# Gate and up units of a feed-forward stage: two of seven products replaced by seven half-size ones, computed one unit ahead

## The chip, the cores and the metric

The kernel runs on one NeuronCore of one Trainium2 chip. The metric is the device time of one execution in microseconds (us). Engines are named as in the profile: PE is the matrix engine, PEld its weight loads, DVE the vector engine, ACT the scalar engine, POOL and SP the two engines that issue most of the transfers here.

## The reference, cut to what matters

The input is 2048 tokens of 512 features, all in f32. One RWKV-like block (time mix, then channel mix) is followed by a gated feed-forward part, and the change lies in the latter:

```python
def _L0_ffn_ref(h_shard, w_gate_up, w_down):
    gate_up = jnp.einsum('bsh,oh->bso', h_shard, w_gate_up)
    gate, up = jnp.split(gate_up, 2, axis=-1)
    h = jax.nn.silu(gate) * up
    out = jnp.einsum('bsi,hi->bsh', h, w_down)
    return out
...
x = x + _L0_attn_ref(_layernorm(x, axis=-1), ...)
x = x + _L0_ffn_ref(_layernorm(x, axis=-1), w_gate_up, w_down)
```

Gate and up have 2048 columns each, so each is four 512 x 512 matrices; down goes from 2048 back to 512.

## The kernel before

Tokens are handled in four blocks of 512. A *unit* is one 512 x 512 weight matrix times one block. It is made with a Strassen-Winograd scheme: weights and activations are cut into 2 x 2 quarters of 256 x 256, sums of quarters are formed (S1 to S4 of the weights, T1 to T4 of the activations), and seven products of quarters replace eight. The seven are, as weight and activation: A11 B11, A12 B21, S2 T2, S1 T1, S3 T3, S4 B22, A22 T4. Each product is four PE matmuls with a 128 x 128 weight and 256 moving columns, and takes one weight tile of 256 KB, which SP loads into `wring`, a ring of 12 tiles, ahead of its use.

`unit` (matmul at L602) runs the products on PSUM banks: `z`, taken from the pool `ps` of six banks, is accumulated over A11 B11, S2 T2, S1 T1, S3 T3 and A22 T4, and read in between; `accv` and `accx` are two banks of their own. ACT copies partial results out (L622 into `accv`, L633 into `u2`, L637 into `accx`), DVE adds them, and `sink` takes each finished quarter: for a gate unit ACT's Silu into a tile `s` (L1169), for an up unit DVE's product with `s` into `hid`. The last three products are not run at once: they go into the list `held`, and the next unit or stage places them between its own products.

The order of all instructions on PE, DVE and ACT is the order in which the Python code issues them. `tick` is called after each product: it counts what DVE has been given, and while there is slack it issues steps of background work: the next block's normalization and transposes (`ffn_in`), sums of hidden quarters (`hidden_done`, `quarter_sums`), and the weight sums (`prepare`). A weight matrix's four sums are prepared once: POOL loads four raw quarters from DRAM, DVE forms S1 to S4, POOL stores them (`prepare`, `prep_one`, `credit`, `pause`); the list `late` gives the order. DVE works in order, so a sum whose raw quarter has not landed holds up what is behind it.

The feed-forward part runs block by block, with gate and up units in turn (`ffn_gate`, `ffn_up`, g = 0 to 3), the next block's first gate unit, and then `ffn_down`. Down uses the scheme twice, one inside the other (`down_product`): 49 products, each of four matmuls with 128 moving columns (L1342). The feed-forward part covers about the span from 655 us to its end.

Of the kernel before, what the change touches and what calls it, by code (L numbers as in the profile page):

```python
# [15 lines left out]
P = 128  # L16
# [4 lines left out]
HB = TB // 2  # L21
# [42 lines left out]
def rwkv_ffn_kernel(  # L64
# [20 lines left out]
    up = ctx.enter_context(tc.tile_pool(name="up", bufs=10))  # L85
    prep = ctx.enter_context(tc.tile_pool(name="prep", bufs=6))
    small = ctx.enter_context(tc.tile_pool(name="small", bufs=3))
    ps = ctx.enter_context(tc.tile_pool(name="ps", bufs=6, space=bass.MemoryType.PSUM))
    pv = ctx.enter_context(tc.tile_pool(name="pv", bufs=1, space=bass.MemoryType.PSUM))
    px = ctx.enter_context(tc.tile_pool(name="px", bufs=1, space=bass.MemoryType.PSUM))  # L90
    dram = ctx.enter_context(tc.tile_pool(name="dram", bufs=1, space=bass.MemoryType.DRAM))


# [16 lines left out]
        return tokp.tile([P, NT, H], F32, tag="tok", name=name)  # L110

    def bank():
        return ps.tile([P, 2, HB], F32, tag="ps", name="ps")

# [29 lines left out]
    def value_part(q, k):  # L146

        if q < 4:
            return wv[q, k].rearrange("p (g c) -> p g c", c=P)
        m, kk = divmod((0, 1, 3, 2)[k], 2)  # L150
        return vsum[q - 4][:, :, kk, m * P : (m + 1) * P]

    for q in (A11, A12, A22, S1, S2, S3, S4):
        sources["vv", q] = [value_part(q, k) for k in range(4)]
# [63 lines left out]
    def value_weight(q, k):  # L218
# [9 lines left out]
        nc.sync.dma_start(t, value_part(q, k))  # L228
        return t

    def load_x(b, queues=None):
        t = tok_tile("x")
        for k in range(NT):
            eng = queues[k] if queues else nc.sync
            paced(eng.dma_start(t[:, k, :], x_t[b][:, k, :]))
        return t
# [54 lines left out]
    preps = deque()  # L291
    credit = [0.0, 0.0]
    pause = [WAIT]

    def prep_one():
        item = preps[0]
        if item[1] > 0:
            return False
        try:
            if next(item[2]) is not None:  # L300
                item[1] = pause[0]
        except StopIteration:
            preps.popleft()
            finished.add(("sums", item[0]))
            if len(preps) > 1 and item[3] > 1:
                begin(preps[1])
            elif preps:
                begin(preps[0])
        return True
# [7 lines left out]
    def prepare_all(ns, own, depth):  # L317
        empty = not preps
        for n in ns:
            preps.append([n, 0, prepare(n, own), depth, False])  # L320
        if empty:
            for item in list(preps)[:depth]:
                begin(item)
# [106 lines left out]
    def tt(out, a, b, op):  # L430
        nc.vector.tensor_tensor(out, a, b, op)  # L431
        cost(size(out))
# [150 lines left out]
    def unit(weights, Bs, sink, by_token, done=None, free=None):  # L583
# [86 lines left out]
        for s in order:  # L670
            if s is None:
                pop_held()
            else:
                s()
                tick()
        held.extend(((STEP, step7), (STEP, step3), (STEP, step4)))

    def plain_unit(n, B, sink, by_token, done=None, free=None, halfway=None, hold=False):

# [451 lines left out]
    def ffn_in(b):  # L1131
# [24 lines left out]
        finished.add((b, "z"))  # L1156
        yield 1
        yield from sums_of(B)

    gated = {}  # L1160

    def ffn_gate(b, g):
        s = gated[b, g] = {}

        tile_of = q_tile if g % 2 else u_tile

        def sink(i, j, c):
            t = tile_of("s")
            nc.scalar.activation(t, c, AF.Silu)  # L1169
            s[i, j] = t  # L1170

        unit([WG + g], [Lazy((b, "z"))], sink, False)

    def ffn_up(b, g):
        s = gated.pop((b, g))
        hid = hidden.setdefault(b, {})

        def sink(i, j, c):
            q = (B11, B12, B21, B22)[2 * i + j]
            if q not in hid:  # L1180
                hid[q] = hidden_tile()
            tt(hid[q][:, g], c, s[i, j], ALU.mult)
            if g == 3:
                made.add((b, q))
                if q in (B11, B22):
                    quarter_sums(b, 0 if q == B11 else 1)

        unit(
            [WU + g],
            [Lazy((b, "z"))],  # L1190
            sink,
            False,
            lambda: hidden_done(b, g),
            op_done if g == 3 else None,
        )
# [38 lines left out]

    def last_room():
        middle.close()
        pools["q"] = ctx.enter_context(
            tc.tile_pool(name="fq", bufs=4, reuse_waits="tile")
        )

    def quarters(t):
        return {2 * k + m: t[:, :, k, m * P : (m + 1) * P] for k in range(2) for m in range(2)}
# [212 lines left out]

    early = [WV, WCR, WO] + [WKEY + g for g in range(4)] + [WVAL, WVAL + 1]
    late = [("vv", q) for q in (A11, S4, S2, A12, S1, S3, A22)]
    late += [n + g for g in range(4) for n in (WG, WU)] + [("dd", A11)]
    late += [("d", k) for k in range(4)] + [("dd", q) for q in (S4, S2, A12, S1, S3, A22)]

    ctx.enter_context(
        tc.manual_schedule(
# [25 lines left out]
    for b in range(NB):  # L1488
# [3 lines left out]
        if b == NB - 1:  # L1492
            load_resid(0)
        if b >= DEEP:
            credit[1], pause[0] = 1.0, LONG
        gate_unit(b)
        if b + 1 < NB:
            out_unit(b + 1)
# [32 lines left out]
                u(b + 2)  # L1531
    credit[1] = 0.75
    need((0, "z"))
    ffn_gate(0, 0)
    last_room()
    for b in range(NB):
        for g in range(4):
            if g > 0:
                need((b, "z"))
                ffn_gate(b, g)  # L1540
            if g == 0 and b + 1 < NB:
                load_resid(b + 1)
            ffn_up(b, g)
            if g == 1 and b + 1 < NB:
                push((b + 1, "z", "t"), ffn_in(b + 1), op_free)
        if b + 1 < NB:
            need((b + 1, "z"))
            ffn_gate(b + 1, 0)
        ffn_down(b)
# [80 lines left out]
```

## Time and profile before

| | |
|---|---|
| median of three runs | 1232.89 us (1231.09 to 1233.88) |
| profiled execution, its own time | 1231.09 us |
| its span, first to last instruction | 1229.0 us |
| PE busy | 1219.5 us, 99% of the span |
| DVE busy | 780.3 us, 63% |
| ACT busy | 368.4 us, 30% |
| moved by DMA | 319.03 MB, mean 260 GB/s |
| granted PE clock | 1.000 |

The page of a profile gives busy time by engine, the span in 40 slices, the chain of work that ended last, and the costliest groups of instructions; a group is a line of the kernel, an engine, an operation and its tiles. A helper that issues all additions (`tt`, L431) gives its line to all of them, so DVE is read by tiles.

### The profile page before, as it was taken

What the parts mean: (1) busy time and instruction counts of PE and PEld (TensorE: products, weight loads), DVE (VectorE), ACT (ScalarE), POOL (GpSimd) and SP (SyncE); (2) the same over time, 40 slices, a digit from 0 to 9 for tenths busy, and PEclk for the clock granted to TensorE, in tenths of its full rate; (3) what the DMA queues carried; (4) which work ended last, traced back from release to release, by engine and by line L of the source; (5) the groups of instructions that cost most, each with busy time, mean ns of one, the idle gap of its engine ahead of it and who ended that gap; (6) DMA issues with size and microseconds to landing.
All of it is one profiled execution on the core that took longest, in us unless ns stands there. A gap on an engine that the chain in (4) does not pass through costs nothing.

```text
span 1229.0 us, 19201 instructions
## 1 busy us (share of the span) xinstructions
PE 1219.5 (99%) x6860; PEld 1106.3 (90%) x6860; DVE 780.3 (63%) x1451; ACT 368.4 (30%) x713; POOL 186.6 (15%) x334
## 2 busy tenths in 40 slices
PE   9999999999999999999999999999999999999998
PEld 8888888888888888998899888998899888998898
DVE  5877686577685666886775577646546364553466
ACT  5534252242532333323412222112221232112211
POOL 2232221223212222002201222200000000000000
PEclk9999999999999999999999999999999999999999
DMA  5768985899888988899889978995469745785576
GB/s 196 250 221 282 319 299 206 302 320 302 277 262 270 312 288 263 261 297 381 280 281 329 335 232 279 362 343 154 146 194 309 258 143 153 250 290 154 153 225 204
DMA packets 159620, 319.03 MB, mean 260 GB/s; under 512 B 19096, under 2 KB 32552, under 8 KB 158248
## 3 DMA queue, kind: packets, MB, share of 16 engines
q1 hardware_dynamic: 132000, 230.22, 58.4%
q0 software_dynamic: 25920, 84.96, 19.0%
q10 hardware_dynamic: 1608, 2.65, 0.7%
q8 instruction: 55, 0.90, 0.3%
q14 instruction: 37, 0.30, 0.1%
HBM read 268.46 MB, written 49.29 MB: 259 GB/s over the span
## 4 chain that ended last, share of the span: by engine, by line
PE 90%; DVE 4%; DMA 3%; ACT 2%; issue 1%; POOL 1%; ACTq 0%; DVEq 0%; POOLq 0%
PE ps L602 45%; PE ps L1342 21%; PE accx L602 9%; PE accv L602 9%; PE ps L704 5%; DMA raw<-in_w 2%; PE ps L487 1%; DMA vsum<-raw 1%; DMA row<-stats 1%; ACT mix L540 1%; DVE raw L431 0%; DVE e L439 0%; DVE h L435 0%; DVE st L445 0%; POOL raw L181 0%
## 5 line engine op out<-in xcount | busy, mean ns | idle before, releaser
L602 PE MATMUL ps<-zT,w 128*128 128x256 f32 x1280 | 289.3, 380 | 0.0
L602 PEld LDWEIGHTS ps<-zT,w 128*128 128x128 f32 x1280 | 242.4, 191 | 31.5
L602 PE MATMUL ps<-mix,w 128*128 128x256 f32 x920 | 211.1, 380 | 1.3 <-ACT u L633 1.3
L602 PEld LDWEIGHTS ps<-mix,w 128*128 128x128 f32 x920 | 174.3, 190 | 24.5 <-ACT u L633 1.7
L1342 PE MATMUL ps<-w,hid 128*128 128x128 f32 x1248 | 156.8, 275 | 0.0
L1342 PEld LDWEIGHTS ps<-w,hid 128*128 128x128 f32 x1248 | 149.7, 192 | 1.2
L1342 PE MATMUL ps<-w,quads 128*128 128x128 f32 x1056 | 133.5, 276 | 0.4 <-ACT r L1354 0.4
L1342 PEld LDWEIGHTS ps<-w,quads 128*128 128x128 f32 x1056 | 126.4, 192 | 1.1 <-ACT r L1354 0.5
L1354 ACT COPY r<-ps 128x128 f32<-128x128 f32 x168 | 44.5, 265 | 204.5 <-PE ps L1342 201.9
L431 DVE TENSOR_TENSOR raw<-raw 128x512 f32<-128x512 f32 x120 | 82.5, 688 | 30.9 <-issue 11.1
L431 DVE TENSOR_TENSOR u<-u,accx 128x512 f32<-128x512 f32 x64 | 43.8, 685 | 85.7 <-ACT accx L637 85.7
L431 DVE TENSOR_TENSOR hid<-hid 128x512 f32<-128x512 f32 x126 | 84.9, 687 | 2.0 <-ACT hid L1068 0.3
L622 ACT COPY accv<-ps 128x512 f32<-128x512 f32 x64 | 36.5, 571 | 158.0 <-PE ps L602 155.2
L637 ACT COPY accx<-ps 128x512 f32<-128x512 f32 x64 | 36.5, 570 | 132.7 <-PE ps L602 126.2
L431 DVE TENSOR_TENSOR u<-ps,u 128x512 f32<-128x512 f32 x64 | 44.2, 690 | 44.5 <-PE ps L602 40.6
L704 PE MATMUL ps<-mix,w 128*128 128x256 f32 x320 | 70.8, 380 | 1.1 <-DVE mix L439 1.1
L633 ACT COPY u<-ps 128x512 f32<-128x512 f32 x64 | 37.4, 584 | 109.5 <-PE ps L602 109.5
L704 PEld LDWEIGHTS ps<-mix,w 128*128 128x128 f32 x320 | 60.4, 191 | 9.5 <-DVE mix L439 1.8
L431 DVE TENSOR_TENSOR r<-ps,r 128x256 f32<-128x256 f32 x83 | 29.8, 359 | 51.5 <-PE ps L1342 47.1
L602 PE MATMUL accv<-zT,w 128*128 128x256 f32 x256 | 60.6, 380 | 0.0
L602 PE MATMUL accx<-zT,w 128*128 128x256 f32 x256 | 60.5, 380 | 0.0
L602 PE MATMUL ps<-w,t 128*128 128x256 f32 x264 | 59.4, 379 | 0.0
(179 smaller groups left out, 1593.7 us busy)
## 6 DMA issues: line engine op xcount, KB each, us to landing
w<-sum SPq DMA_DIRECT2D x248, 256.0 KB, 4.2
w<-in_w SPq DMA_DIRECT2D x230, 256.0 KB, 4.2
w<-dd SPq DMA_DIRECT2D x112, 256.0 KB, 3.8
w<-vsum SPq DMA_DIRECT2D x56, 256.0 KB, 4.4
w<-vv SPq DMA_DIRECT2D x56, 256.0 KB, 4.0
raw<-in_w POOLq DMA_DIRECT2D x48, 256.0 KB, 6.7
w<-d SPq DMA_DIRECT2D x48, 256.0 KB, 3.5
sum<-raw POOLq DMA_DIRECT2D x40, 256.0 KB, 4.1
```

Of the source, the lines that this page charges most:

```text
L431: nc.vector.tensor_tensor(out, a, b, op)
L487: nc.tensor.transpose(flat[:, t * P : (t + 1) * P], h[:, t, c * P : (c + 1) * P], ident)
L540: nc.scalar.activation(dst(c), hT[:, c, 0:TB].rearrange("p (j t) -> p j t", j=2), AF.Copy, scale=onem[:, row - MK, c : c + 1],)
L602: mm = nc.tensor.matmul(pz[:, m, :], lhsT=lhsT, rhs=rhs, start=first and g == 0 and m == 0 and k == 0, stop=g == last and k == 1, skip_gro ...
L622: "z", A11, B11, True, pop_held, read=lambda: nc.scalar.copy(accv, acc["z"])
L633: nc.scalar.copy(tmp["u2"], acc["z"])
L637: nc.scalar.copy(accx, acc["z"])
L704: mm = nc.tensor.matmul(acc[i, j][:, m, :], lhsT=act[:, k, lo] if by_token else wg[:, k, lo], rhs=wg[:, k, :] if by_token else act[:, k, : ...
L1342: mm = nc.tensor.matmul(dst, lhsT=x[k][:, g, :], rhs=wt[:, g, :], start=first and g == 0, stop=g == 3, skip_group_check=True,)
L1354: nc.scalar.copy(st["r"][:, m, n * P : (n + 1) * P], st["z"])
```

## The change

Of the gate and up units, all but the first gate and the first up of block 0 get their A11 B11 and S3 T3 from a new function, `inner`. Instead of two products of four matmuls with 256 moving columns it makes seven of the same scheme one level down, each with half the size: two matmuls with 128 moving columns, one for A11 B11 and one for S3 T3, which lie side by side in a bank. The seven go into two banks of `ps` (`z`: A11, S2, S1, S3, A22; `y`: A12, S4), are read into a tile `pair` by ACT (`keep`) and joined by DVE (`joined`, and an addition in `five`). They are cut into five steps (`one` to `five`), and `paired_unit` places one (a call of `small`) in front of each of its own products, one unit ahead: while unit u runs its five remaining products, it makes the two results that unit u+1 needs. At its end ACT writes the finished A11 B11 of the next unit from `pair` into the banks `z` and `accv`, where the next unit's products add to it; S3 T3 (`plus`) is added by DVE when a quarter is taken. Only one product (`last`: S4 B22) is held over.

Around it: `z` and a new bank `w` become fixed banks (`acc2`), for which `ps` is left with four banks in the feed-forward part; inner sums of the activations are formed by DVE (`inner_sums`), inner sums of the weights by four more `prepare` items (`("in", ...)`); each inner step needs four weight tiles in place of two; a prepare item's loads may begin while the one before it is at work (`AHEAD`); `ffn_in` of the next block is pushed one pair of units earlier; the order `late`, and some credits, change.

The core of the diff:

```diff
-    ps = ctx.enter_context(tc.tile_pool(name="ps", bufs=6, space=bass.MemoryType.PSUM))
     pv = ctx.enter_context(tc.tile_pool(name="pv", bufs=1, space=bass.MemoryType.PSUM))
     px = ctx.enter_context(tc.tile_pool(name="px", bufs=1, space=bass.MemoryType.PSUM))
+    ps = ctx.enter_context(tc.tile_pool(name="ps", bufs=4, space=bass.MemoryType.PSUM))
+    extra = ctx.enter_context(ExitStack())
+    banks = [
+        ps,
+        ps,
+        extra.enter_context(tc.tile_pool(name="ps2", bufs=2, space=bass.MemoryType.PSUM)),
+    ]
...
+        banks.append(banks.pop(0))
+        return banks[-1].tile([P, 2, HB], F32, tag="ps", name="ps")
...
+    def inner_weight(n, q):
+        t = WG if n < WU else WU
+        need_sums(("in", t, q))
+        r = wring.tile([P, 2, HB], F32, tag="w", name="w").rearrange("p a (h c) -> p (a h) c", c=P)
+        nc.sync.dma_start(r, insums[t, q][:, :, n - t, :])
+        return r
...
+            item[5] += 1
+            if item[5] == AHEAD[0] and item[3] == 1 and len(preps) > 1:
+                begin(preps[1])
...
+        def act(i, k):
+            wanted = ("in", tcol[k]) if k in tcol else T3
+            while wanted not in B["sums"]:
+                run_one(True)
+            if k in tcol:
+                return B["in"][:, i, tcol[k], :]
+            k, j = divmod(k, 2)
+            return B[(B11, T3)[i]][:, k, j * P : (j + 1) * P]
...
+        def mm(dst, q, k, start):
+            for i in range(2):
+                m = nc.tensor.matmul(
+                    dst[:, i, :],
+                    lhsT=wt(i, q),
+                    rhs=act(i, k),
+                    start=start and i == 0,
+                    stop=True,
+                    skip_group_check=True,
+                )
+            latest[:] = [m.ins.name]
+        def keep(m, j):
+            nc.scalar.copy(st["r"][:, :, m, j * P : (j + 1) * P], st["z"])
+        def one():
+            st["r"] = pair_tile()
+            st["w"] = [weight(n, A11), weight(n, S3)]
+            st["s"] = [inner_weight(n, A11), inner_weight(n, S3)]
+            st["z"] = flat(bank())[:, :HB].rearrange("p (i c) -> p i c", i=2)
+            st["y"] = bank().rearrange("p i (j c) -> p i j c", j=2)
+            mm(st["z"], A11, B11, True)
+            keep(0, 0)
+            mm(st["y"][:, :, 0, :], A12, B21, True)
+            tick(2 * HALF)
+        def two():
+            mm(st["z"], S2, T2, False)
+            keep(1, 0)
+            tick(HALF)
+        def three():
+            mm(st["z"], S1, T1, False)
+            keep(0, 1)
+            mm(st["y"][:, :, 1, :], S4, B22, False)
+            later(joined, 1)
+            tick(2 * HALF)
+        def joined():
+            r = st["r"]
+            tt(r[:, :, 1, :P], r[:, :, 1, :P], r[:, :, 0, P:], ALU.subtract)
+            tt(
+                r[:, :, 0, :],
+                st["y"].rearrange("p i j c -> p i (j c)"),
+                r[:, :, 0, :],
+                ALU.add,
+            )
+        def four():
+            mm(st["z"], S3, "T3", False)
+            keep(1, 1)
+            tick(HALF)
+        def five():
+            mm(st["z"], A22, T4, False)
+            r = st["r"]
+            tt(r[:, :, 1, :P], st["z"], r[:, :, 1, :P], ALU.add)
+            tick(HALF)
...
+        z, aw = acc2["z"], acc2["w"]
+        plus = None if st is None else st["r"][:, 1]
+        u2 = None
+        small()
+        pop_held()
+        if st is None:
+            product(z, A11, B11, True)
+            nc.scalar.copy(accv, z)
+            tick()
+            pop_held()
+        small()
+        product(z, S2, T2)
+        if st is None:
+            u2 = u_tile("u2")
+            nc.scalar.copy(u2, z)
+        else:
+            nc.scalar.copy(aw, z)
+        tick()
+        pop_held()
+        small()
+        product(accv, A12, B21)
+        sink(0, 0, accv)
+        tick()
+        if st is None:
+            plus = bank()
+            product(plus, S3, T3, True)
+            tt(u2, plus, u2, ALU.add)
+            plus7 = u_tile("p7")
+            nc.scalar.copy(plus7, plus)
+            plus = plus7
+            tick()
+        small()
+        product(z, S1, T1)
+        nc.scalar.copy(accx, z)
+        sink(1, 1, z, plus)
+        tick()
+        small()
+        product(aw, A22, T4, st is None)
+        sink(1, 0, aw, plus if u2 is None else u2)
+        if after is not None:
+            r = ahead[after[0]][0]["r"][:, 0]
+            nc.scalar.copy(z, r)
+            nc.scalar.copy(accv, r)
+        tick()
+        def last():
+            product(accx, S4, B22)
+            sink(0, 1, accx)
+            if free is not None:
+                free()
+            if done is not None:
+                later(done, 1)
+        held.append((STEP, last))
...
+        sums = (
+            (x(0, 1), x(0, 0)),
+            (x(1, 1), new[:, :, 0, :]),
+            (x(1, 0), new[:, :, 1, :]),
+            (x(1, 1), x(0, 1)),
+        )
+        for k, (i0, i1) in enumerate(sums):
+            tt(new[:, :, k, :], i0, i1, ALU.subtract)
+            B["sums"].add(("in", k))
+            yield
...
+        def sink(i, j, c, plus=None):
+            t = u_tile("s")
+            if plus is not None:
+                tt(t, c, plus, ALU.add)
+                c = t
             nc.scalar.activation(t, c, AF.Silu)
             s[i, j] = t
-        unit([WG + g], [Lazy((b, "z"))], sink, False)
+        if (b, g) == (0, 0):
+            unit([WG + g], [Lazy((b, "z"))], sink, False)
+            return
+        paired_unit((b, g, 0), b, WG + g, following(b, g, 0), sink)
...
+            h = hid[q][:, g]
+            if plus is not None:
+                tt(h, c, plus, ALU.add)
+                c = h
+            tt(h, c, s[i, j], ALU.mult)
...
-    late += [n + g for g in range(4) for n in (WG, WU)] + [("dd", A11)]
-    late += [("d", k) for k in range(4)] + [("dd", q) for q in (S4, S2, A12, S1, S3, A22)]
+    late += [n + g for n in (WG, WU) for g in range(4)]
+    late += [("in", n, q) for q in (A11, S3) for n in (WU, WG)] + [("dd", A11)]
+    late += [("d", k) for k in range(4)] + [("dd", q) for q in (A12, S4, S2, S1, S3, A22)]
...
-            credit[1], pause[0] = 1.0, LONG
+            credit[1], pause[0], AHEAD[0] = 0.75, LONG, 2
...
+    banks[:] = [ps]
...
-            if g == 1 and b + 1 < NB:
+            if g == 0 and b + 1 < NB:
                 push((b + 1, "z", "t"), ffn_in(b + 1), op_free)
+            credit[1] = 0.45 if g in (0, 1) else 0.75
```

In `joined` the sums of the scheme's second level are formed; `following` names the next gate or up unit, `None` after the last one, and gates alternate with ups except where a down stage lies between.

## Prediction

> **What bounds the kernel now.** I read the page's head and its chain first, to see which engine sets the end.
>
> ```profile
> PE 1219.5 (99%) x6860; PEld 1106.3 (90%) x6860; DVE 780.3 (63%) x1451; ACT 368.4 (30%) x713; POOL 186.6 (15%) x334
> PE 90%; DVE 4%; DMA 3%; ACT 2%; issue 1%; POOL 1%; ACTq 0%; DVEq 0%; POOLq 0%
> ```
>
> PE is busy 99% of the span and makes 90% of the chain. A microsecond less of PE work is a microsecond of the end, as long as PE does not begin to wait. The chain in order of time, at the end of block 2's units, shows what each product costs (start, length, line, records; a product is 8 records).
>
> ```profile
> 1026.24 1.73 PE accv L602 x8
> 1027.97 1.73 PE ps L602 x8
> 1043.51 3.45 PE ps L602 x16
> 1046.97 0.89 PE ps L1342 x8
> 1047.86 1.73 PE ps L602 x8
> ```
>
> A product with 256 moving columns takes 1.727 us (accv to ps: 1027.97 - 1026.24), one with 128 takes 0.893 us (39.30 us for the 352 records from 1054.83). A unit is seven of the former, 12.09 us, with no gap. Then the timeline (start, length), for how soon a reader starts, and for PE after a wait:
>
> ```profile
> 963.90 1.89 PE L602 MATMUL accv<-zT,w 128*128 128x256 f32 x8
> 964.10 0.69 DVE L431 TENSOR_TENSOR hid<-ps,s 128x512 f32<-128x512 f32 x1 [2.17 <-PE ps L602]
> 965.63 1.89 PE L602 MATMUL ps<-zT,w 128*128 128x256 f32 x8
> 965.89 0.60 ACT L1169 ACTIVATE s<-accv 128x512 f32<-128x512 f32 x1 [2.94 <-PE accv L602]
> ```
>
> Counted from the start of PE's next product, DVE reads the last one's result after 0.20 us, ACT after 0.26. Where PE waited for ACT (423.95 us, 1.29 us of waiting) it restarted 0.05 us after ACT's copy ended. Groups by form give the other durations, and the windows the DMA (20 us each; the last two numbers are the busy share and GB/s).
>
> ```profile
> L622 ACT COPY accv<-ps 128x512 f32<-128x512 f32 x64 | 36.5, 571 | 158.0 <-PE ps L602 155.2
> L1169 ACT ACTIVATE s<-u 128x512 f32<-128x512 f32 x16 | 10.1, 632 | 8.6 <-DVE u L431 8.6
> L836 ACT COPY row<-ps 4x256 f32<-4x256 f32 x2 | 0.7, 358 | 0.0
> L431 DVE TENSOR_TENSOR u<-ps,u 128x512 f32<-128x512 f32 x64 | 44.2, 690 | 44.5 <-PE ps L602 40.6
> L431 DVE TENSOR_TENSOR r<-ps,r 128x256 f32<-128x256 f32 x42 | 17.9, 425 | 4.4
> ```
>
> ```profile
> 560.00:580.00 20.00, 20.00 (x95) 17.64 (x94) 10.87 (x19) 6.71 (x12) 5.84 (x11) 1.00 1.03 392
> 640.00:660.00 20.00, 20.00 (x163) 19.54 (x162) 15.08 (x28) 3.87 (x13) 1.08 (x2) 1.00 0.88 296
> 660.00:680.00 20.00, 20.00 (x98) 17.75 (x97) 8.11 (x13) 5.41 (x10) 5.90 (x11) 1.00 0.99 368
> 680.00:700.00 20.00, 20.00 (x94) 17.66 (x93) 9.42 (x15) 4.67 (x8) 4.84 (x9) 1.00 0.95 328
> ```
>
> **PE's own work.** 30 of the 32 gate and up units change; the built order shows 180 matmuls more, 30 x (14 - 8), so the edit does what it says. Removed: 2 x 1.727 = 3.454 us a unit. Added: 7 pairs of half a 128-column product, 7 x 0.4465 = 3.126 us. The difference is 0.328 us, times 30: **-9.8 us**. Bounds: if a pair cost just a quarter of 1.727 us, -12.9; if each of the five groups of small matmuls cost 0.03 us at its border (one product behind a 0.89 us one shows 1.76 us for 1.73), -5.3. I take -9.8, as behind other 0.89 us products PE shows 1.73 unchanged.
>
> **A new wait, from a gate unit to the up unit behind it.** Follow ACT's queue at the end of a gate unit, from the end of product A22 T4, called 0. DVE adds `plus` to bank `w` (0.20 to 0.89), ACT takes Silu of that (+0.05, 0.63: 1.57), and only behind it in ACT's order stand the two seeds, `copy(z, r)` and `copy(accv, r)` (0.57 each: 2.71) and the `keep` of step `one` (0.36: 3.07). Step `two` of the up unit overwrites what `keep` reads, so PE may start it at 3.12. PE meanwhile has step `one` (0.89) and `last` (1.73), that is 2.62. It waits 0.50 us, and all that follows in its queue with it. Behind an up unit ACT's seeds need only `five`'s addition, no Silu: about 2.1 us, hidden under the same 2.62, and with half a microsecond to spare; that cover gone, a further DVE step in front would cost up to 0.7 us. Where a down stage follows the gate unit, PE has 3.5 us of products first, and nothing is lost. So 12 places: g = 1, 2, 3 in four blocks, 11 x 0.50 and one, without a unit behind the up unit, of 0.46: **+6.0 us**.
>
> DVE makes it worse where background work stands in front of that addition. DVE is free 0.62 us before point 0 (S1 T1 ended 2.17 us before; +0.26 and 0.57 for ACT's copy to `accx`, 0.69 for the addition to `z`), and `five`'s addition needs 0.425. In the built order of the changed kernel the steps placed between are: block 0, one weight sum; one with three tiny steps (0.16 each); two weight sums. Blocks 1 and 2: one BNStats and its aggregate (0.67 + 0.18), then two sums of `zT` (0.69 each), then none. Block 3: none. The addition starts late by 0.30, 0.78, 0.99; 0.46, 0.99; 0.46, 0.99: **+5.0 us**. Lower bound 0, if DVE's steps ran in gaps; upper about 8, with one more step in half the places.
>
> A seed from SBUF into PSUM is in no row; the nearest are 0.57 (PSUM to PSUM) and 0.63 (Silu from SBUF). I took 0.57; 0.63 adds 1.4 us in all. The Trainium skill, "ScalarE: Activation LUTs", Rules for kernel authors, budgets about 0.3 us an ACTIVATE plus 0.83 ns an element, 0.73 us for 512 columns and 0.51 for 256; the rows show 0.57 and 0.36, and by the page the waits would cost some 5.5 us more.
>
> **Four banks for transposes.** The next block's 16 transposes ran in one stretch of 1.75 us. Now the third group of four needs the first group's bank: evacuation starts 0.26 after that group, takes 0.605 (the `zT` copy), +0.05, against 0.44 us of the second group: 0.48 us, three times: **+1.4 us**. In the down stage a product's two banks come back two products later; I cost that at nothing, since DVE's joins there end one product later (0.89 us each); without it a product would wait some 0.4 us.
>
> **Transfers in block 0.** A unit loads nine tiles in place of seven: 2.36 MB in 11.8 us, 200 GB/s where it was 152. In blocks 1 to 3 the windows stand at 136 to 157 GB/s, so that is free. In block 0 the weight sums of down run beside it, and since a unit now has more ticks, they are issued sooner: counted in the built order, 24.4 MB stand beside PE's 640 to 700 us, where it was 19.4 (the windows show 19.8). That is 406 GB/s; the highest window moved 392. 24.4 MB at 392 take 62.2 us, 2.2 more than 60, and loads stand only about 7.4 us ahead of their use (from the release of a ring tile), with landings of 4.0 to 7.5 us in this stretch. I take **+2.5 us**, near the 2.2. The lower end is 0 (the ring hides it; more bytes can't gain). The upper is 11.3, where DVE's stalls come on top: it works in order, and raw quarters issued only 3 to 6 us ahead land after 6.4; in before it lost 9.1 us so, with no wait on PE. The skill's page "DMA: Bandwidth & Descriptors", Specifications, gives a limit of about 358 GB/s for a core; by it those bytes would take 68 us and the term would be 8. The window of 392 speaks against the page.
>
> **At nothing.** Four more weight sums (16 x 0.69 us of DVE) lie before the feed-forward part, where DVE is busy 11 to 16 of 20 us and PE does not wait; at most 2 us. The first paired up unit has its seven large products as before. The additions DVE gains (in a gate unit 2.9 us in place of 1.4) fit: it was busy 47 of 95 us in block 1's units.
>
> **Sum.** -9.8 + 6.0 + 5.0 + 1.4 + 2.5 = +5.1 us. The profiled execution took 1231.09 us, 2.1 beside its span; so 1236.2 on its footing. It is the lowest of three runs; the median, 1232.89, is 1.8 higher, and the forecast for a median is 1238.0. About 0.2%, or 2.5 us, is what a measurement of this kernel can tell from no change.
>
> **Rivals.**
> Faster: `two` does not wait, because ACT's four items take 0.5 us less than their rows or Silu comes early, and DVE's steps in front run in gaps. For it: PE has not waited once in these units, and ACT is busy 30%. Against it: ACT works in order, and every duration is a row. It decides from a chain under 2.62 us. Then -9.8 + 1.4 + 2.5 = -5.9: 1227.0. Chance 0.20.
> No change: the wait is the bare 0.50 us, DVE's background steps cost nothing. Then +0.1: 1233.0. Chance 0.18.
> Forecast, 1238: chance 0.42.
> Much slower: block 0 is held by transfers, or DVE by raw quarters, until the ring is dry; for it the 0.99 share of 660 to 680, against it that raw waits were harmless before. It decides if more than 392 GB/s is asked for longer than the ring lasts. The term is 11.3 in place of 2.5: 1246.8. Chance 0.20.
>
> The range cuts the outer rivals in their middle, half of 0.20 on either side: 1227 to 1247. Alone the forecast's own range is 1234 to 1242. Faster has rival one, 0.20; within 0.2% lies most of the second, 0.17; the rest is slower, 0.63.
>
> **What would show it.** PE busy near 1210 us with PE waiting: "PE ... <- ACT" about 0.5 to 1.5 us at 11 places before step `two`, nothing behind up units. Windows of block 0 over 380 GB/s. If PE's waits in blocks 1 to 3 sum to under 3 us, the chain was wrong; if a pair of small matmuls takes over 0.47 us, the first term was; if PE waits for DMA in block 0 by more than 5 us, the transfers were undersized.

## The result, and the profile after

The changed kernel takes 1279.17 us (median of four, 1277.6 to 1282.7) against 1231.99 us for the kernel before: the ratio is 1.0387, with a 95% interval of 1.0357 to 1.0416. It is 47 us slower; the forecast was 5 us slower, and its range ended at 1247. The profiled execution took 1282.71 us, and its span is 1280.9 us, 51.9 us more than before. First the page's head, its slices and its chain:

```profile
PE 1230.7 (96%) x7220; PEld 1117.4 (87%) x7220; DVE 835.7 (65%) x1574; ACT 422.9 (33%) x864; POOL 207.9 (16%) x366
...
PEclk9999999999999999998998898999999999999999
...
PE 71%; DMA 9%; DVE 8%; issue 7%; ACT 3%; POOL 1%; SPq 0%; POOLq 0%; ACTq 0%; DVEq 0%
```

PE was to fall from 1219.5 to about 1210 us and shows 1230.7, and its idle time grew from 9.5 to 50.2 us (span less busy). The clock row, all nines before, has four slices below 9. All four lie between 576 and 801 us, in the end of the attention part and in block 0, and PE's share of the chain fell from 90 to 71%. The view of PE's waits (total, times, longest) names who was late:

```profile
PE ps L753 <- ACT pair L764: 7.8, 9, 2.9
PE ps L1613 <- DVE r L471: 7.0, 1, 7.0
PE accx L642 <- DVE u L471: 5.5, 1, 5.5
PE accz L836 <- DMA w<-sum: 5.0, 1, 5.0
PE accx L836 <- DMA w<-sum: 4.5, 2, 2.7
PE ps L753 <- DVE zT L471: 3.9, 1, 3.9
PE ps L753 <- DVE inner L471: 3.9, 1, 3.9
```

Only the first row is the wait that the forecast worked out. The others are DVE late with something and ring loads late, and the page does not say yet what DVE was doing. The timeline does. Here are POOL's and DVE's rows between 684 and 698 us:

```profile
684.23 0.54 POOL L220 DMA_DIRECT2D d<-raw  x1 [7.22 <-DVE raw L471]
...
687.27 0.54 POOL L209 DMA_DIRECT2D raw<-in_wd  x1 [1.71 <-issue]
688.93 0.54 POOL L209 DMA_DIRECT2D raw<-in_wd  x1 [1.12 <-DMA d<-raw]
690.85 1.21 POOL L209 DMA_DIRECT2D raw<-in_wd  x2 [1.37 <-DMA d<-raw]
...
697.54 0.69 DVE L471 TENSOR_TENSOR raw<-raw 128x512 f32<-128x512 f32 x1 [9.10 <-DMA raw<-in_wd]
```

The four raw loads of one item of weight sums do not leave together. In front of three of them stand two waits of POOL, until stores of the item before have landed and set raw tiles free, and the last two leave at 690.9. DVE had come to that item's first sum at 688.4 and stood in order until 697.54. PE stood here too, from 689.6 to 694.58, but for a ring load (the row `accz` of the waits, 5.0 us); behind DVE's late addition it then lost 1.42 us more. In the down stage of block 0 DVE's stand is PE's wait:

```profile
823.33 0.54 POOL L209 DMA_DIRECT2D raw<-in_wd  x1 [3.00 <-DMA dd<-raw]
829.87 1.42 DVE L471 TENSOR_TENSOR raw<-raw 128x512 f32<-128x512 f32 x2 [10.41 <-DMA raw<-in_wd]
831.59 0.42 DVE L471 TENSOR_TENSOR r<-ps,r 128x256 f32<-128x256 f32 x1
832.07 5.09 PE L1613 MATMUL ps<-w,hid 128*128 128x128 f32 x24 [6.98 <-DVE r L471]
```

The last load of the item leaves behind a store, DVE stands for 10.41 us, the addition to `r` stands behind it, and PE waits 6.98 us for that. In the kernel before, the four loads of the item that begins at 661.56 left in one row, and DVE came to its sums 8 us later, without a wait:

```profile
661.56 2.13 POOL L181 DMA_DIRECT2D raw<-in_wd  x4 [3.02 <-PE ps L602]
669.82 2.13 DVE L431 TENSOR_TENSOR raw<-raw 128x512 f32<-128x512 f32 x3
670.80 0.55 POOL L192 DMA_DIRECT2D d<-raw  x1 [7.11 <-DVE raw L431]
```

What PE pays beyond standing still is in windows of 4 us (busy time of PE, PEld, DVE, ACT and POOL, granted clock, DMA share, GB/s):

```profile
692.00:696.00 4.00, 1.42 (x3) 1.18 (x4) 0.00 (x0) 0.00 (x0) 1.13 (x3) 0.66 1.07 344
696.00:700.00 4.00, 2.58 (x7) 1.57 (x6) 2.43 (x4) 1.14 (x3) 1.47 (x3) 0.50 1.06 385
700.00:704.00 4.00, 4.00 (x14) 3.41 (x15) 2.47 (x5) 1.32 (x3) 0.67 (x2) 0.56 0.99 323
```

After the wait the granted clock is 0.5, and at 704 us it is back at 1.0; the first eight matmuls after it (694.58) take 3.78 us in place of 1.89. Over all such windows, busy time times (1 - clock) sums to 13.9 us; in the kernel before it is 0. So the span's 51.9 us are -9.8 (PE's own work, as forecast), +40.7 of idle time, +13.9 of slow clock, and some 7 us left over. PE lists 27 waits, where it listed 7 in the kernel before; if each costs 0.27 us beyond its idle time, as the gate to up wait below does, the 20 more make 5 of these 7, which no run shows by itself.

By place: the first product of the feed-forward part starts at 665.8 us, where it was 655.0 (+10.8, some 8 of it one wait of 5.5 us that begins at 591 us, while DVE stands 7.6 us for a raw quarter of a new item, `raw<-third`, and the slow clock behind it). The down stage of block 0 ends at 864.3 us where it ended at 816.5, which is another 37.0 us for block 0. From there to PE's last product, blocks 1 to 3 together take 3.7 us longer.

### The profile page after: what moved, and what is told of

It reads as the page before. It is cut to its first block, busy times and chain, and to the rows that moved or that the text cites. A ratio compares the mean times of both kernels' runs of the same rounds, so it can differ in the third digit from the quotient of the medians.

```text
span 1280.9 us, 20346 instructions
## 1 busy us (share of the span) xinstructions
PE 1230.7 (96%) x7220; PEld 1117.4 (87%) x7220; DVE 835.7 (65%) x1574; ACT 422.9 (33%) x864; POOL 207.9 (16%) x366
## 4 chain that ended last, share of the span: by engine, by line
PE 71%; DMA 9%; DVE 8%; issue 7%; ACT 3%; POOL 1%; SPq 0%; POOLq 0%; ACTq 0%; DVEq 0%
PE ps L642 20%; PE ps L1613 16%; PE accz L836 7%; PE ps L753 6%; PE ps L928 4%; PE accx L642 4%; PE accv L642 4%; PE accv L836 4%; PE accw L836 2%; PE accx L836 2%; DMA w<-sum 2%; DMA d<-raw 2%; DMA raw<-in_wd 2%; DMA raw<-in_w 1%; PE ps L527 1%
## 5 line engine op out<-in xcount | busy, mean ns | idle before, releaser
L471 DVE TENSOR_TENSOR raw<-raw 128x512 f32<-128x512 f32 x136 | 93.5, 688 | 77.1 <-DMA raw<-in_wd 29.1
L836 PE MATMUL accz<-zT,w 128*128 128x256 f32 x504 | 124.6, 392 | 5.2 <-DMA w<-sum 5.0
L836 PEld LDWEIGHTS accz<-zT,w 128*128 128x128 f32 x504 | 94.4, 197 | 16.8 <-DMA w<-sum 5.2
L753 PEld LDWEIGHTS ps<-inner,w 128*128 128x128 f32 x480 | 72.2, 195 | 23.4 <-ACT pair L764 13.8
L753 PE MATMUL ps<-inner,w 128*128 128x128 f32 x480 | 75.9, 282 | 12.1 <-ACT pair L764 7.8
L764 ACT COPY pair<-ps 128x256 f32<-128x256 f32 x120 | 44.6, 371 | 68.6 <-PE ps L753 68.6
L471 DVE TENSOR_TENSOR r<-r 128x128 f32<-128x128 f32 (+1 forms) x83 | 40.2, 486 | 30.5 <-ACT r L1625 29.2
L836 PE MATMUL accw<-zT,w 128*128 128x256 f32 x248 | 60.0, 386 | 0.0
L1709 POOL DMA_DIRECT2D out<-resid x12 | 8.6, 715 | 313.5 <-DVE resid L471 287.9
```

What stands on the lines that cost most here:

```text
L753: m = nc.tensor.matmul(dst[:, i, :], lhsT=wt(i, q), rhs=act(i, k), start=start and i == 0, stop=True, skip_group_check=True,)
L764: nc.scalar.copy(st["r"][:, :, m, j * P : (j + 1) * P], st["z"])
L836: mm = nc.tensor.matmul(dst[:, m, :], lhsT=wg[:, kk, m * P : (m + 1) * P], rhs=act[:, kk, :], start=start and m == 0 and kk == 0, stop=kk ...
L1709: eng.dma_start(out_t[b][:, tokens, cols], rs[b][:, tokens, cols])
```

## Experiments

Theory A: the change brings four more items of weight sums (`in`), and begins items early to make up for it; loads then wait for stores, DVE stands on landings, PE behind DVE, and the clock drops. Rival B: transfers. Rival C: the paired unit itself. Differences between medians below carry 2 to 3 us, since the kernel before moved by up to 1.9 us between groups of runs.

**No early begin.**

```diff
-            credit[1], pause[0], AHEAD[0] = 0.75, LONG, 2
+            credit[1], pause[0], AHEAD[0] = 0.75, LONG, 9
```

> The changed kernel, but an item of weight sums is no longer begun while its predecessor still has two sums to make (AHEAD stays 9); all else, the bytes and the paired units, as changed. Theory A (early begin: two of the next item's four raw loads must wait on POOL's queue for stores of the item before, the pause counted in ticks is over before they have landed, DVE stands in order on a raw quarter, PE behind DVE, and PE's granted clock is halved for some 4 us after each wait of about 3 us or more): DVE's waits for raw<-in_wd fall from 29 us to 5 to 12, PE's idle time from 50 to 15 to 25 us, 1240 to 1258 us. Rival B (transfers: block 0 asks for more bytes than the queues move): the bytes are the same, so 1272 to 1284. Rival C (the paired unit itself: additions on DVE, seeds on ACT, waits at gate to up): 1275 to 1284.

Measured: 1331.17 us, ratio 1.0804 (1.0760 to 1.0847). All three missed. DVE's waits for `raw<-in_wd` did fall, to 11.8 us, and the wait at 591 was gone, but the items now came too late for the products that load their results, those of the down stage (`dd`) and one of block 0's first units (`third`):

```profile
PE ps L1613 <- DMA w<-dd: 52.6, 6, 11.5
PE ps L642 <- DMA w<-third: 20.3, 1, 20.3
```

So the early begin is not the fault by itself: it saves 52 us of a larger loss. The items stand in a line with a due time, the down stage of block 0.

**The kernel before with the four items alone**, made at their place in the order and used by nobody:

```diff
-    late += [n + g for g in range(4) for n in (WG, WU)] + [("dd", A11)]
+    late += [n + g for g in range(4) for n in (WG, WU)]
+    late += [("in", n, q) for q in (A11, S3) for n in (WU, WG)] + [("dd", A11)]
```

> The kernel before with the four new items of weight sums made at their place in the order (ahead of the down sums) and used by nobody; no paired unit, no early begin, pause and credit as before. If the four items alone push the down sums too late, the down stage of block 0 waits for its ring loads as in the run without early begin: 1245 to 1285 us. If their loss needs the paired unit (its shorter ticks or its ring loads): 1232 to 1238.

Measured: 1299.63 us, ratio 1.0545 (1.0525 to 1.0565), more than either expectation. There is no paired unit in this kernel, its first feed-forward product starts at 657.3 us, and its loss is mostly one row (PE is busy 13.9 us longer as well, with the granted clock down to 0.5 behind these waits):

```profile
PE ps L1363 <- DMA w<-dd: 50.7, 7, 12.6
```

In the kernel before, an item begins every 18.3 us in block 0 (loads at 661.56 for the first, 771.42 for the seventh). Four more in front put the line some 73 us back, and the down stage of block 0, which had its sums just in time, waits. In this run the item that began at 661.56 begins at 740.76:

```profile
740.76 2.13 POOL L202 DMA_DIRECT2D raw<-in_wd  x4 [0.86 <-PE ps L623]
```

So the four items alone lose more than the whole change does. The changed kernel wins part of that back by the early begin: 36 raw loads stand in its feed-forward part, where there were 28, two items more and not four.

**The kernel before with the early begin alone** (and its item A12 put first among the down sums, as that begin needs):

```diff
+            if item[5] == AHEAD[0] and item[3] == 1 and len(preps) > 1:
+                begin(preps[1])
...
-            credit[1], pause[0] = 1.0, LONG
+            credit[1], pause[0], AHEAD[0] = 1.0, LONG, 2
```

> The kernel before with the early begin alone (AHEAD 2 from the third block on) and the item A12 of the down sums put first, as that begin needs; no paired unit, ticks as before, so a pause of six ticks is 10 us here and about 7 in the changed kernel. Theory A: the loads wait for stores here as well, but the longer pause covers part of it: 1236 to 1258 us with DVE's waits for raw quarters of 15 to 30 us. Rival B: bytes as before, 1231 to 1235. Rival C: 1231 to 1235.

Measured: 1257.55 us, ratio 1.0192 (1.0165 to 1.0219): the early begin costs 25 us without any paired unit, as A says and B and C do not. Nearly all of it falls before the feed-forward part (its first product is at 680.4 us, 25.4 later): PE waits 7.4, 3.5 and 2.6 us there, each for DVE and each with the clock down behind it. Behind that block 0 takes 2.1 us longer than in the kernel before, so the early begin by itself does not make the 37 us there.

**Seven raw tiles for six:**

```diff
-    prep = ctx.enter_context(tc.tile_pool(name="prep", bufs=6))
+    prep = ctx.enter_context(tc.tile_pool(name="prep", bufs=7))
```

> The changed kernel with seven raw tiles for weight sums in place of six (all that there is room for), so that of an early item one load and not two waits for a store. Theory A: DVE's waits for raw quarters in block 0 fall by a quarter to a half, 1262 to 1277 us. Rivals B and C: 1277 to 1284, since neither bytes nor the paired units change.

Measured: 1267.5 us, ratio 1.0282 (1.0247 to 1.0317). One tile more, no byte fewer, and 12 us are back; DVE's waits for `raw<-in_wd` fall from 29.1 to 12.5 us. That loads wait for stores, at this price, is shown by this.

**What the down items cost in block 0, taken out in three steps.** First DVE's additions of these items run on a spare tile:

```diff
+            if isinstance(n, tuple) and n[0] in ("d", "dd"):
+                tt(spare, spare, spare, op)
+            else:
                 tt(o, i0, i1, op)
```

> The changed kernel, but the 40 additions on DVE of the down weight sums read and write one spare tile, and the raw quarters are stored back as they came (so the down weights are not sums and the result is not the reference's). Loads, stores, bytes, POOL's queue and DVE's busy time stay; only DVE no longer stands on a raw quarter's landing. Theory A' (DVE, in order, stands on raw quarters in block 0, PE behind it, and the clock behind PE): PE's waits for DVE and ACT over 1 us in block 0 go, the clock stays at 1.0 there, what stays is the wait at 591 and a wait for ring loads of a few us: 1245 to 1258 us. Rival B (transfers): PE waits for ring loads instead, 1265 us or more. Rival C: 1275 to 1284.

Measured: 1267.45 us, ratio 1.0290 (1.0273 to 1.0308), 12 us back. A was too hopeful: DVE no longer stands on a landing in block 0, yet the two waits of 3.9 us for `zT` and `inner` remain, with the clock down behind both. They come from DVE's time: the sums take the place of the next block's norm, which then has to be made in one stretch while PE stands.

Then the additions are left out altogether; loads and stores stay:

```diff
-            tt(o, i0, i1, op)
+            if not (isinstance(n, tuple) and n[0] in ("d", "dd")):
+                tt(o, i0, i1, op)
```

> The changed kernel without the 40 additions on DVE of the down items; their raw quarters are loaded and stored back as they came (so the down result is not the reference's). All transfers stay, DVE neither stands on raw quarters nor spends 27 us on them, and the steps of block 1's norm no longer stand behind them. If DVE's room is what block 0 lacks: the two waits of 3.9 us at block 1's first operands and the gate to up waits over 1 us go with their clock drops, a ring wait of 3 to 6 us stays, 1246 to 1257 us. If it is the transfers: ring waits of 10 us or more, 1260 or more.

Measured: 1257.51 us, ratio 1.0202 (1.0184 to 1.0220), 10 us more back, half a microsecond above what the first of the two expected. The two waits are gone, and ring waits of 9.8 us are left (two in block 0, at its start, in windows that move up to 401 GB/s, and one in each of blocks 1 and 2):

```profile
PE accx L837 <- DMA w<-sum: 5.5, 3, 2.1
PE accz L837 <- DMA w<-sum: 4.3, 1, 4.3
...
684.00:700.00 16.00, 11.72 (x55) 10.14 (x55) 3.19 (x5) 3.18 (x7) 5.03 (x10) 0.91 1.04 401
```

Then the items' transfers go too:

```diff
-            need_sums(("dd", q))
-            src = sums["dd", q][k - 4]
+            src = wd[q % 4, k - 4]
...
-    late += [("in", n, q) for q in (A11, S3) for n in (WU, WG)] + [("dd", A11)]
-    late += [("d", k) for k in range(4)] + [("dd", q) for q in (A12, S4, S2, S1, S3, A22)]
+    late += [("in", n, q) for q in (A11, S3) for n in (WU, WG)]
```

> The changed kernel without the ten items of weight sums of the down stage: down loads raw quarters in place of their sums (so the down result is not the reference's); 40 raw loads, 40 sums on DVE and 40 stores of block 0 are gone, the ring's loads and all of PE's work stay. Theory A: block 0's waits and clock drops go with them; left are PE's own -9.8 us, the gate to up waits of 1 to 1.5 us a block, about 1 us at transposes, 4.5 us of waits for ring loads in blocks 1 and 2, and the wait of 5.5 us at 591 with its clock drop: 1230 to 1243 us. Rival B: the same, 1228 to 1240. Rival C: over 1260 us, PE's idle time stays at 40 us or more.

Measured: 1247.59 us, ratio 1.0112 (1.0084 to 1.0139), another 10 us; above the range of A, and C is out. Block 0 (first product to the end of its down stage) now takes 1.8 us longer than in the kernel before, in place of 37. So its loss, by the three steps in this order: 12 us of DVE standing on landings, 10 of DVE's time, 10 of transfers, each with its share of slow clock (by block 0's own length in the profiles, 13, 14 and 9).

**Without the four new items** (the small products load raw quarters of the same size in their place):

```diff
-        need_sums(("in", t, q))
...
-        nc.sync.dma_start(r, insums[t, q][:, :, n - t, :])
+        nc.sync.dma_start(r, w[n, 0 if q == A11 else 1])
...
-    late += [("in", n, q) for q in (A11, S3) for n in (WU, WG)] + [("dd", A11)]
+    late += [("dd", A11)]
```

> The changed kernel without the four items of weight sums that are new (16 loads, 16 sums, 16 stores); the small products load raw quarters of the same size in their place (so gate and up are not the reference's), all of PE's work stays. Theory A'' (the four items push the down sums some two items further into block 0, so that they have to be made faster there): the wait at 591 goes (9 to 11 us), and block 0 loses half or more of its 37 us, 1236 to 1256 us. If only the early begin counts and not the number of items, block 0 still loses 30 us or more, and 1262 to 1275 us comes out.

Measured: 1255.61 us, ratio 1.0199 (1.0174 to 1.0224). The four items account for 24 us of the changed kernel's loss, and 24 us are left without them. The early begin is still in force, and PE waits 3 times for 2.8 to 3.1 us in block 0. The wait at 591 falls from 5.5 to 1.7 us, but three waits there still delay the feed-forward part by 6.9 us. Block 0 still takes 15.2 us longer than in the kernel before, though only 20 raw loads stand in its feed-forward part, where there were 28. So a longer line is not all of it. The early begin without paired units costs block 0 2.1 us, and paired units without down items cost it 1.8 us; early begin, paired units and these 20 loads together cost 15.2. No run has the paired units in block 0 with neither the four items nor the early begin, so how these 15 us split is open.

**The seeds ahead of the addition and the Silu**, on the kernel without down sums:

```diff
-        sink(1, 0, aw, plus if u2 is None else u2)
         if after is not None:
             r = ahead[after[0]][0]["r"][:, 0]
             nc.scalar.copy(z, r)
             nc.scalar.copy(accv, r)
+        sink(1, 0, aw, plus if u2 is None else u2)
```

> The changed kernel without the ten down items (their sums replaced by raw quarters, as in the run without down sums), and with the two seeds put ahead of the addition and the Silu of the same step in ACT's order. Theory: the gate to up waits of 0.55, 1.08 and 0.63 us a block vanish, 8 us in all against the run without down sums: 1238 to 1241 us. If the wait is set by the addition and not by ACT's order: 1245 to 1248.

Measured: 1241.90 us, ratio 1.0082 (1.0063 to 1.0100), 5.7 us less than without the edit (3.7 by the ratios, as the kernel before was 1.9 us faster in that group of runs) and just above the range of the theory. The row of PE's waits for `keep` showed 4.3 us in 9 waits, the longest 0.8; with the edit it is

```profile
PE ps L751 <- ACT pair L762: 1.1, 3, 0.4
```

Three of twelve places keep some 0.36 us. So most of the wait from gate to up is ACT's order, as forecast.

**Ring waits in blocks 1 and 2.** First another queue for the residual and x of blocks 2 and 3:

```diff
-        paced(nc.sync.dma_start(r, resid[b]))
-        loads[b] = r, load_x(b)
+        eng = nc.gpsimd if b >= 2 else nc.sync
+        paced(eng.dma_start(r, resid[b]))
+        loads[b] = r, load_x(b, (eng,) * NT)
```

> As the run without down sums and with the seeds ahead (1241.9 us), but blocks 2 and 3 load their residual and x on POOL's queue in place of SP's, so they no longer stand in front of the ring's loads. If the waits of 1.9 and 2.2 us for ring loads in blocks 1 and 2 come from SP's queue they vanish: 1236 to 1239 us. If they come from the bytes, they stay: 1240 to 1244.

Measured: 1240.18 us, ratio 1.0055 (1.0033 to 1.0077); the waits stay at 2.5 and 1.9 us. It is not the order on SP's queue. Then x a gate and up pair later than the residual:

```diff
-        loads[b] = r, load_x(b)
+        loads[b] = r,
...
+            loads[0] += (load_x(0),)
...
+            if g == 1 and b + 1 < NB:
+                loads[b + 1] += (load_x(b + 1),)
             ffn_up(b, g)
-            if g == 0 and b + 1 < NB:
+            if g == 1 and b + 1 < NB:
                 push((b + 1, "z", "t"), ffn_in(b + 1), op_free)
```

> The run without down sums and with the seeds ahead (1241.9 us; down loads raw quarters, so its result is not the reference's), and x loaded a gate and up pair later than the residual, the norm begun after the second up unit. If the two ring waits at the start of blocks 1 and 2 (1.9 and 2.2 us, some 5 with the drain and the clock) come from that burst: 1236 to 1238.5 us, with PE's waits for w<-sum under 0.5 us. Otherwise 1240 to 1243.

Measured: 1243.58 us, ratio 1.0079 (1.0060 to 1.0098). No ring wait is left, so it was the burst, but the time did not fall, since the norm began later and PE now waits for its result once in each block:

```profile
PE ps L751 <- DVE zT L469: 7.3, 3, 2.5
```

The burst is easily missed: the forecast read 136 to 157 GB/s in blocks 1 to 3, but at a block's start the residual and x (2 MB) fall together with the ring. Windows of 16 us there, first of the kernel before, then of the changed one, whose units load nine tiles in place of seven:

```profile
952.00:968.00 16.00, 16.00 (x83) 14.33 (x82) 4.46 (x8) 3.74 (x8) 0.73 (x2) 1.00 0.98 360
```

```profile
1004.00:1020.00 16.00, 14.27 (x97) 13.25 (x97) 9.21 (x17) 4.57 (x11) 1.43 (x2) 1.00 1.02 367
```

**Paired units only where there is room.** First from gate 2 of block 1 on, with the four items beside the down stage of block 0:

```diff
+    START = (1, 2)
...
-        if (b, g) == (0, 0):
+        if (b, g) < START:
             unit([WG + g], [Lazy((b, "z"))], sink, False)
...
+    late += [("in", n, q) for n in (WU, WG) for q in (A11, S3)]
```

> Paired units only from gate 2 of block 1 on (19 units gain 0.33 us each); block 0 and the attention part as in the kernel before, with its order of weight sums, its pause and credit and no early begin; the four new items are made last, beside the down stage of block 0; the two seeds stand ahead of the addition and Silu on ACT. All computed. Theory A: no loss before 1.2, no wait at gate to up: 1232.9 - 6.2 + 0.9 (transposes) + 0 to 4 (ring loads) = 1226 to 1232 us. Rival B: the paired units' extra ring loads cost in blocks 1 to 3 as well, 1234 to 1242. Rival C: paired units are slower in themselves, 1238 or more.

Measured: 1252.56 us, ratio 1.0173 (1.0158 to 1.0189), a miss for A and B; C's range holds it, but the runs below, with 15 of these units, are not slower than the kernel before. Everything up to the end of block 0's units was as before (first feed-forward product at 656 us), but in its down stage, where the four items now stood, DVE came late with `quads` and `hid` (4.7 and 3.1 us of PE's time), and the next block's norm came late behind that. DVE itself stood 7.37 us up to 800.43 on a raw quarter of the new items. Then from block 2 on, with the items in block 1's units:

```diff
-    START = (1, 2)
+    START = (2, 0)
...
-    late += [("in", n, q) for n in (WU, WG) for q in (A11, S3)]
...
         ffn_down(b)
+        if b == 0:
+            prepare_all([("in", n, q) for n in (WU, WG) for q in (A11, S3)], True, 1)
```

> Paired units in blocks 2 and 3 only, everything up to there in the order of the kernel before; the four new items are made in block 1's units, where the windows show 136 to 157 GB/s and DVE is half idle; seeds ahead of the addition, residual and x of block 3 on POOL's queue. All computed. Theory: 15 units gain 0.33 us each (-4.9), transposes cost 0.5 to 0.9, one gate to up place 0.6 in each block: 1228 to 1232 us. If the paired unit costs by itself: 1233 to 1240.

Measured: 1231.66 us, ratio 0.9993 (0.9981 to 1.0005). A ring wait of 2.1 us at the start of block 2, with 1.4 us of slow clock behind it, took back much of the 4.9 us that 15 paired units gain. With the edit of the run with x later, on top of this:

> The run with pairs from block 2 on (1231.7 us), but the next block's x (four loads of 256 KB) is loaded a gate and up pair later than its residual (1 MB), and its norm begins after the second up unit; both on SP's queue. If the ring wait of 2.1 us at 970, and the 1.4 us of clock behind it, come from 2 MB that fall together with nine tiles a unit into one stretch at 390 GB/s, they go: 1227 to 1229.5 us, ratio 0.996 to 0.998. If the wait comes from elsewhere: 1231 to 1233.

Measured: 1231.72 us, ratio 0.9994 (0.9984 to 1.0003). The ring wait went and a wait of 2.4 us for `zT` came, as in the kernel without down sums. Then x half a pair earlier and the norm a unit earlier:

```diff
             if g == 1 and b + 1 < NB:
-                loads[b + 1] += (load_x(b + 1),)
-            ffn_up(b, g)
-            if g == 1 and b + 1 < NB:
                 push((b + 1, "z", "t"), ffn_in(b + 1), op_free)
+            ffn_up(b, g)
+            if g == 0 and b + 1 < NB:
+                loads[b + 1] += (load_x(b + 1),)
```

> As the run with x later and pairs from block 2 on (1231.7 us), but x is loaded half a pair earlier, behind the first up unit, and the next block's norm begins one unit earlier, ahead of the second up unit. If the wait of 2.45 us at the next block's first operands comes only from the later start of that norm, it goes and no ring wait returns: 1227 to 1230 us, ratio 0.995 to 0.998. If loads and norm can't both have room, one of the two waits is back: 1231 to 1233. All computed.

Measured: 1229.48 us, ratio 0.9986 (0.9977 to 0.9995): faster than both kernels, by 0.14% of the one before, an interval that leaves out 1 by little. No wait of PE in its feed-forward part exceeds 0.36 us, the clock is at 1.0 wherever PE works, and PE is busy for 1215.9 us, 3.6 less than in the kernel before.

## Why the prediction was right or wrong

**PE's own work, -9.8 us: right.** An `accz` product takes 1.73 us (1190.24 - 1188.51 in the timeline), the small one behind it 0.44, and a whole unit 11.76 us (from 1176.75 to 1188.51), as forecast:

```profile
1188.51 1.89 PE L836 MATMUL accz<-zT,w 128*128 128x256 f32 x8
1190.24 0.61 PE L753 MATMUL ps<-inner,w 128*128 128x128 f32 x4
```

Its check by the page's busy time ("near 1210") failed all the same, since busy time grows with a slow clock.

**The gate to up wait, +11.0 us in two terms: right in mechanism, 3 of 11 us too large.** The worst of three places in block 1, up to PE's restart:

```profile
913.10 0.68 DVE L471 TENSOR_TENSOR s<-accw,pair 128x512 f32<-128x512 f32 x1
...
913.81 0.63 ACT L1418 ACTIVATE s<-s 128x512 f32<-128x512 f32 x1 [1.63 <-DVE s L471]
914.35 0.58 ACT L888 COPY accz<-pair 128x512 f32<-128x512 f32 x1
914.87 0.58 ACT L889 COPY accv<-pair 128x512 f32<-128x512 f32 x1
...
915.38 0.36 ACT L764 COPY pair<-ps 128x256 f32<-128x256 f32 x1
915.79 0.71 PE L753 MATMUL ps<-inner,w 128*128 128x128 f32 x4 [0.81 <-ACT pair L764]
```

Silu, two seeds and `keep` stand in the order that was worked out, and the seed's unknown duration is 0.58, between the bounds of 0.57 and 0.63. But items that show 0.63 and 0.58 follow each other after 0.51 to 0.54, and DVE's addition was 0.7 us late where 0.99 was forecast. PE lists 0.28, 0.81 and 0.36 us in blocks 1 and 2; counted from the start of the product in front to the end of the small one, the places cost 0.55, 1.08 and 0.63, each 0.27 more than its row lists. Unhindered products overlap (1.89 us long, 1.73 apart), and a wait breaks that; how the 0.27 comes about is not shown further. With 1.25 in block 3 and block 0 as the run without down sums shows it, that is 3 x 2.26 + 1.25 = 8.0 us. Turning the order round won 5.7 us (3.7 by the ratios). The Trainium skill, "ScalarE: Activation LUTs", Rules for kernel authors, gives its 0.3 us for a bias that is a pointer operand; by it, as an estimate, the seed would take 0.73 us, and the row says 0.58.

**Transposes, +1.4: right.** In the run without down sums PE lists 0.24 us at each of three, which with the restart is 0.46 in the start times.

**Transfers in block 0, +2.5 us, at most 11.3: this step failed.** Its place and its pieces were right: 381 GB/s from 680 to 700, DVE standing in order on raw quarters, a dry ring, and the forecast's own sign of it, over 5 us of PE's waits for DMA in block 0, came with 5.01. But it is 32 us by the three steps above, of which only 10 are transfers. The forecast counted the weight sums of down, which are issued sooner, only as bytes (24.4 MB for 19.4); it did not follow the items as a line, in which each item waits for the tiles of the last and the down stage waits for the end. Its last rival, "much slower", is the case that came, at a chance of 0.20; the 11.3 us that it set for it are a third of the 32.

**At nothing: four more items ahead of the feed-forward part, "at most 2 us": this failed too**, and it is the root of 24 of the 47 us. Priced as 16 additions in DVE's free time, the items bring 32 transfers and 73 us of line, and the run without them is 24 us faster. In front of the feed-forward part the changed kernel loses 10.8 us, 6.9 of them in the run without these items too, where the early begin is still in force.

**No term for the clock.** Every wait was priced at its length. The six stretches of slow clock in the changed kernel cost 1.3 to 3.5 us each, on top of the waits in front of them.

**In blocks 1 to 3, ring loads "free": wrong by 4.5 us** of listed waits. The forecast's 136 to 157 GB/s are not all of its windows there: the kernel before moved 208 GB/s from 820 to 840 us, and 360 in the 16 us from 952, which became 367 in the changed kernel, with PE waiting.

## What to carry to other kernels

Work that is made ahead for a later stage is a line with a due time: before pricing more of it, take the pace from the trace (here 18.3 us an item) and count how far it moves the last one, whatever share of each engine it uses. A load issued early is early only if its tile is free; behind a store that has not landed it waits, and an engine that works in order then stands for it. A gain of 0.33 us a unit is worth having only where the stage has room in DVE and in transfers, which a window of some 16 us shows and an average over a block does not.

## What the runs showed of the hardware

The granted clock fell after single waits, and not at a fixed length: after 5.01 and 2.88 us (changed kernel), 2.14 us (pairs from block 2) and 1.95 us (other queue) windows of 4 us show 0.5 to 0.6, while after 2.75 us (875 us, changed kernel) it stayed at 1.0. The run with x later on the kernel without down sums has three listed waits of 2.45 us: behind two of them (756 and 901 us) it fell to 0.62 and 0.57, behind the third (1045 us) it did not. So the "about 3 us or more" of the first expectation is no bound. The Trainium skill, "TensorE: Matmul & The Clock Gate", has half rate after about 3.4 us of idle time (Part 1) and advises against gaps of over 3 us ("Why this matters for your kernels"); the half rate agrees, while the runs show it after listed gaps of 2 us.

A row's idle time understates a wait of PE: in block 1 of the changed kernel a listed 0.28 us cost 0.55 and a listed 0.81 us cost 1.08.
